# A graph-attention layer on one core: products and sums of a node group's end with one operand in PSUM

## The chip, the cores and the metric

The kernel runs on one core of one Trainium2 chip. The core has a matrix engine (TensorE, PE in the profile), a vector engine (VectorE, DVE), a scalar engine (ScalarE, ACT), a general engine (GpSimd, POOL) and a synchronisation engine (SyncE, SP) that issues most of the transfers. Each engine runs its own instructions in order; semaphores order the engines among themselves. SBUF is the working memory, PSUM the memory that TensorE writes its results to, in banks of 512 f32 columns on 128 partitions. GpSimd issues the indirect transfers, which fetch rows from main memory by a list of row numbers.

The metric is the device time of one execution in microseconds.

## The reference

12500 nodes with 128 features, 400000 edges sorted by destination, 8 heads of 16 channels. Cut to what matters:

```
h  = relu(layernorm(x))
xl, xr = ln(h) @ W_l, ln(h) @ W_r
m  = leaky_relu(xl[src] + xr[dst] + edge_attr @ W_e, 0.2)     # edges and one self loop for each node
alpha = sum(m * att, over the channels of a head)
a  = softmax of alpha over the edges of one destination and head
h  = h + sum(a * xl[src], over those edges) + bias
ff = gelu(ln(h) @ W1 + b1) @ W2 + b2
out = x + h + ff
```

The self loop uses the mean of edge_attr over all edges in place of an edge's own.

## The kernel before, in words

A first stage (lines 334 to 376) goes over 14 groups of seven node tiles, writes xl and xr to main memory and keeps h in SBUF (`h_sb`), with the bias added.

The second stage (`window_edges`) goes over the edges. A unit is 256 edges, a pair two units, 512 edges; there are 782 pairs. The work is software-pipelined by hand: one pass of the loop at line 931 is a round, and in round r each stage function handles the pair r minus its offset (table at line 868). For one pair:

- `gather` (line 517): four indirect transfers on GpSimd's queue fetch 128 rows of xl each into `xs`, one of 12 row buffers. There are 3125 of them in all.
- `combine` (559 to 563): TensorE transposes the rows into `z` and adds the destinations' part and the edges' part.
- `slope`, `bend` (569, 574): the leaky ReLU, ScalarE and VectorE, result `m` in SBUF.
- `score` (580, 581): the negated scores into `ab`, with large values where an edge doesn't belong to a node.
- `lowest`, `weigh` (588, 599): the minimum on VectorE, then exponentials on ScalarE into `p`.
- `turn`, `keep_turned` (607, 612): p transposed by TensorE, copied by ScalarE.
- `collect` (621): weighted sums of rows into a PSUM tile `acc`.
- `own_heads` (630, 636) and `put` (643): each head's own columns, written as a record to the `state` arrays in main memory.

PSUM has eight banks, and the pool `ps2` uses them all: two each for z, ab, pt_ps and acc. A tile of a name takes the two banks of that name in turn. A stage that asks for a bank waits until the last reader of its previous holder is done.

The third part is the node groups' end. The 98 node tiles are cut into 25 groups, one of two tiles and 24 of four, so an instruction over a group has 128 partitions x 512 columns. When all edges of a group are done, its steps (table at line 893) run one or two to a round beside the edge pairs' stages, at the end of the round. A group starts at the earliest 23 rounds after the one before it; the first starts in round 199, the last in round 790, after all edges. `bank_of` (line 676) gives a step a bank of the ring `acc`. The steps that the change touches, in order:

- `f_den` (740): weights of the two state records and of the self loop, divided by their sum, into `wt` (SBUF).
- `f_out` (750): products, two of the records' sums by their weights (line 755) and one of the self loop's rows by theirs (759).
- `f_add` (765): the three products are added up (767, 768).
- `f_h` (770): the sum is added to h (772), and the load of x is issued on SP's queue (773).
- `f_stats`, `f_root`, `f_scale`, `f_turn`, `f_turned` (775 to 818): layer norm of h, transposed; at its end x gets b2 added (818).
- `f_up`, `f_gelu` (820 to 842): the first layer of the feed forward, in two halves.
- `f_x` (844): x gets h added (846).
- `f_down`, `f_store` (848 to 866): the second layer, x plus its result (863), and the store.

The order of the round at line 931: `early`, the pair stages in the order of their table, the loads of the edge mean, the group's steps, then loads and record writes. Each engine's queue has that order.

Of the kernel before, what the change touches and what calls it, by code (L numbers as in the profile page):

```python
# [13 lines left out]
F32 = mybir.dt.float32  # L14
# [7 lines left out]
P = 128  # L22
H = 8
C = P // H
# [21 lines left out]
GN = 4  # L46
# [47 lines left out]
def node_groups(nt):  # L94

    first = nt % GN
    return ([(0, first)] if first else []) + [(t, GN) for t in range(first, nt, GN)]
# [19 lines left out]
def tile_gnn(  # L117
# [261 lines left out]
    with tc.If(fast == 1) as cmp:  # L379
        window_edges(  # L380
            tc, n_edges, ea_t, NT, NE, NUE, ident, wer, we_z, negrep, diag, nid, farw, b2_r, w1_sb, w2_sb, cols,
            xl_dram, xl_t, xr_t, xs_dram, dc_dram, du_dram, state, x_t, out_t, h_sb, src_sb, first_sb,
        )
# [67 lines left out]
def window_edges(  # L451
# [9 lines left out]
    nc = tc.nc  # L461
    SP = mybir.EngineType.SP
    KP = UP * KU
    EPR = UP * U
    AHEAD = 4
# [17 lines left out]
    with ExitStack() as es:  # L483
# [4 lines left out]
        ps2 = es.enter_context(tc.tile_pool(name="e_ps2", bufs=2, space=PSUM))  # L488

        fin = es.enter_context(tc.tile_pool(name="e_fin", bufs=1))  # L490
# [155 lines left out]
        sums = [None] * NL  # L646
# [23 lines left out]
        groups = [{"t0": t, "n": n, "ts": slice(t, t + n)} for t, n in node_groups(NT)]  # L670

        def tiles(name, d, tag=None, bufs=1):
            d[name] = fin.tile([P, GN, P], F32, name=f"f_{name}", tag=tag or f"f_{name}", bufs=bufs)
            return d[name][:, 0 : d["n"]]

        def bank_of(d, name):
            d[name] = ps2.tile([P, EPR], F32, name="acc")
            return d[name]

        def f_load(d):  # L680
# [16 lines left out]
        def f_z(d):  # L697

            n, z = d["n"], bank_of(d, "z")
            for i in range(n):  # L700
                nc.tensor.matmul(
                    z[:, i * P : (i + 1) * P], d["xl"][:, i, 0:P], ident, start=(i == 0), stop=False, is_transpose=True
                )
            for i in range(n):
                nc.tensor.matmul(z[:, i * P : (i + 1) * P], d["xr"][:, i, :], ident, start=False, stop=(i == n - 1))
# [9 lines left out]
        def f_score(d):  # L715

            n, sc = d["n"], bank_of(d, "sc")
            for i in range(n):
                nc.tensor.matmul(
                    sc[:, i * H : (i + 1) * H], d["m"][:, i, :], negrep[:, 0, :], start=(i == 0), stop=(i == n - 1)  # L720
                )
# [18 lines left out]
        def f_den(d):  # L740
            n, wt = d["n"], d["wt"]
            ws = fin.tile([P, 2, GN * H], F32, name="f_ws")[:, :, 0 : n * H]
            nc.vector.tensor_mul(ws, wt[:, 0:2], d["sums"][:, :, :, C])
            den = fin.tile([P, GN * H], F32, name="f_den")[:, 0 : n * H]
            nc.vector.tensor_add(den, ws[:, 0], ws[:, 1])
            nc.vector.scalar_tensor_tensor(den, den, 1e-16, wt[:, 2], op0=OP.add, op1=OP.add)
            nc.vector.reciprocal(den, den)
            nc.vector.tensor_mul(wt, wt, den[:, None].to_broadcast([P, 3, n * H]))

        def f_out(d):  # L750
            n, wt = d["n"], d["wt"]
            o = fin.tile([P, 2, GN * H, C], F32, name="f_o", tag="big", bufs=3)
            d["o"] = o.rearrange("p s (t h) c -> p s t (h c)", h=H)[:, :, 0:n]
            for i in range(2):
                nc.vector.tensor_mul(
                    o[:, i, 0 : n * H], d["sums"][:, i, :, 0:C], wt[:, i, :, None].to_broadcast([P, n * H, C])
                )
            o2 = tiles("o2", d, "f_a")
            nc.vector.tensor_mul(
                o2.rearrange("p t (h c) -> p (t h) c", c=C),  # L760
                d["xo"][:, 0:n].rearrange("p t (h c) -> p (t h) c", c=C),
                wt[:, 2, :, None].to_broadcast([P, n * H, C]),
            )

        def f_add(d):
            o = d["o"]
            nc.vector.tensor_add(o[:, 0], o[:, 0], o[:, 1])
            nc.vector.tensor_add(o[:, 0], o[:, 0], d["o2"][:, 0 : d["n"]])

        def f_h(d):  # L770
            hb = h_sb[:, d["ts"], :]
            nc.vector.tensor_add(hb, hb, d["o"][:, 0])
            nc.sync.dma_start(tiles("x", d), x_t[:, d["ts"], :])

        def f_stats(d):
# [27 lines left out]
        def f_turn(d):  # L803
            tp = bank_of(d, "tp")
            for i in range(d["n"]):
                nc.tensor.transpose(tp[:, i * P : (i + 1) * P], d["hn"][:, i, :], ident)

        def f_turned(d):
            n = d["n"]
            nc.scalar.activation(  # L810
                tiles("hT", d, "f_d").rearrange("p t f -> p (t f)"),
                d["tp"][:, 0 : n * P],
                AF.Identity,
                bias=cols[:, 3:4],
                scale=cols[:, 2:3],
            )
            x = d["x"][:, 0:n]
            nc.vector.tensor_add(x, x, b2_r[:, None, :].to_broadcast([P, n, P]))

        def f_up(k):  # L820
            def up(d):
                n, u = d["n"], bank_of(d, f"u{k}")
                nc.tensor.matmul(  # L823
                    u[:, 0 : n * P],
                    w1_sb[:, k * P : (k + 1) * P],
                    d["hT"][:, 0:n].rearrange("p t f -> p (t f)"),
                    start=True,
                    stop=True,
                )

            return up

        def f_gelu(k):
            def gelu(d):
                n = d["n"]
                if k == 0:
                    d["gel"] = fin.tile([P, 2, GN * P], F32, name="gel", tag="big", bufs=3)
                nc.scalar.activation(
                    d["gel"][:, k, 0 : n * P], d[f"u{k}"][:, 0 : n * P], AF.Gelu, bias=cols[:, 5 + k : 6 + k]
                )  # L840

            return gelu

        def f_x(d):
            x = d["x"][:, 0 : d["n"]]
            nc.vector.tensor_add(x, x, h_sb[:, d["ts"], :])

        def f_down(d):
            y = bank_of(d, "y")
            for i in range(d["n"]):  # L850
                for k in range(2):
                    nc.tensor.matmul(  # L852
                        y[:, i * P : (i + 1) * P],
                        d["gel"][:, k, i * P : (i + 1) * P],
                        w2_sb[:, k, :],
                        start=(k == 0),
                        stop=(k == 1),
                    )

        def f_store(d):  # L860
            n = d["n"]
            y = tiles("yo", d, "f_b")
            nc.vector.tensor_add(
                y, d["x"][:, 0:n], d["y"][:, 0 : n * P].rearrange("p (t f) -> p t f", f=P)
            )
            nc.sync.dma_start(out_t[:, d["ts"], :], y)

        stages = (
# [20 lines left out]
            (3, mean),  # L889
        )  # L890
        SUM_STEP = 2
        early = ((18, f_gelu(1)),)
        steps = (
            (0, f_load),
            (1, f_order),
# [3 lines left out]
            (5, f_low),  # L899
            (6, f_exp),  # L900
            (7, f_den),
            (8, f_out),
            (9, f_add),
            (10, f_h),
            (11, f_stats),
            (12, f_root),
            (13, f_scale),
            (14, f_turn),
            (15, f_turned),
            (16, f_up(0)),  # L910
            (17, f_up(1)),
            (17, f_gelu(0)),
            (18, f_x),
            (19, f_down),
            (20, f_store),
        )
        GAP = 23
        last_round = n_pr + LATE + 2
# [5 lines left out]
        def in_round(r, table):  # L924
            for k, f in table:
                for d in groups:
                    if d["round"] + k == r:
                        f(d)

        with tc.manual_schedule():  # L930
            for r in range(-AHEAD, max(last_round, groups[-1]["round"] + 21)):
                in_round(r, early)
                for late, f in stages:
                    c = r - late
                    if 0 <= c < n_pr:
                        f(c)
                for late, f in sum_stages:
                    i, off = divmod(r - late, SUM_STEP)
                    if off == 0 and 0 <= i < NL:
                        f(i)  # L940
                in_round(r, steps)
                for late, f in late_stages:
                    c = r - late
                    if 0 <= c < n_pr:
                        f(c)
# [335 lines left out]
```

## Time and profile before

| | us |
|---|---|
| median of 3 runs | 4345.91 |
| lowest, highest | 4344.86, 4346.41 |
| the profiled execution's own time | 4342.05 |
| its span, first to last instruction | 4340.7 |

Mean granted TensorE clock in the span: 0.940.

What the engines are busy with in the stretch in which node groups and edge pairs run side by side (columns: stretch in us, its length, then busy us and count of PE, PE's weight loads, VectorE, ScalarE and GpSimd, the clock, the share of the transfer engines, GB/s):

```profile
1310.00:4282.00 2972.00, 2632.88 (x13704) 1831.05 (x13821) 1660.21 (x3624) 1328.46 (x2683) 2257.84 (x2324) 0.96 0.57 112
```

The vector instructions of the group's end, by line (count of full groups, busy us, mean ns of one, idle time before them):

```profile
L755 DVE TENSOR_TENSOR f_o<-st,f_wt 128x512 f32<-128x512 f32 x48 | 30.8, 682 | 0.0
...
L768 DVE TENSOR_TENSOR f_o<-f_o,f_o 128x512 f32<-128x512 f32 x24 | 16.6, 692 | 0.8
...
L818 DVE TENSOR_TENSOR f_x<-f_x,b_r 128x512 f32<-128x512 f32 x24 | 16.4, 684 | 0.0
L846 DVE TENSOR_TENSOR f_x<-f_x,h_sb 128x512 f32<-128x512 f32 x24 | 16.4, 683 | 0.0
L759 DVE TENSOR_TENSOR f_o<-f_xo,f_wt 128x512 f32<-128x512 f32 x24 | 16.4, 682 | 0.0
L772 DVE TENSOR_TENSOR h_sb<-h_sb,f_o 128x512 f32<-128x512 f32 x24 | 16.4, 681 | 0.0
```

Such a row reads: the source line, the engine, the operation, the tile written and the tiles read, their shape, the count; then the sum of durations, the mean of one, and how long the engine had been idle just before such instructions, with what ended that. Seven lines (one of them with two instructions a group) of some 0.68 us each make about 131 us of VectorE's 2453.7.

### The profile page before, as it was taken

What the parts mean: (1) busy time and instruction counts of PE and PEld (TensorE: products, weight loads), DVE (VectorE), ACT (ScalarE), POOL (GpSimd) and SP (SyncE); (2) the same over time, 40 slices, a digit from 0 to 9 for tenths busy, and PEclk for the clock granted to TensorE, in tenths of its full rate; (3) what the DMA queues carried; (4) which work ended last, traced back from release to release, by engine and by line L of the source; (5) the groups of instructions that cost most, each with busy time, mean ns of one, the idle gap of its engine ahead of it and who ended that gap; (6) DMA issues with size and microseconds to landing.
All of it is one profiled execution on the core that took longest, in us unless ns stands there. A gap on an engine that the chain in (4) does not pass through costs nothing.

```text
span 4340.7 us, 65036 instructions
## 1 busy us (share of the span) xinstructions
PE 3622.3 (83%) x18449; PEld 2499.6 (58%) x18571; DVE 2453.7 (57%) x5415; ACT 1837.8 (42%) x3826; POOL 3140.2 (72%) x3244
## 2 busy tenths in 40 slices
PE   0558888888888888889888889888888888888996
PEld 0335565556556556666666566566666665665664
DVE  4755665656665555555555555555555555555554
ACT  0643333333334444444444444444444444444443
POOL 0567777777777777777777777777777777777773
PEclk9768999999999999999999999999999999999998
DMA  7456766766665555565555555555555555555552
GB/s 193 142 158 143 161 150 156 152 153 157 150 151 104 118 112 112 112 119 111 113 111 115 115 102 113 117 112 119 113 113 119 110 112 110 110 112 108 110 114 60
DMA packets 644020, 538.41 MB, mean 124 GB/s; under 512 B 381797, under 2 KB 533605, under 8 KB 643413
## 3 DMA queue, kind: packets, MB, share of 16 engines
q1 hardware_dynamic: 512212, 299.56, 28.6%
q0 software_dynamic: 100000, 217.80, 28.6%
q10 hardware_dynamic: 31440, 16.80, 1.6%
q8 instruction: 152, 2.49, 0.2%
q14 instruction: 216, 1.76, 0.2%
HBM read 473.99 MB, written 59.76 MB: 123 GB/s over the span
## 4 chain that ended last, share of the span: by engine, by line
PE 40%; DMA 23%; POOL 20%; issue 12%; ACT 2%; ACTq 2%; DVE 2%; SPq 0%; POOLq 0%; DVEq 0%
DMA xs<-xl_dram,src_sb 22%; POOL xs L517 20%; PE z L563 9%; PE acc L621 8%; PE ab L581 6%; PE z L559 4%; PE pt_ps L607 4%; PE z L562 2%; PE lr L363 2%; ACTq L334 1%; PE ab L580 1%; PE acc L852 1%; PE acc L823 1%; ACT h_sb L348 0%; ACT xlr L364 0%
## 5 line engine op out<-in xcount | busy, mean ns | idle before, releaser
L517 POOL DMA_INDIRECT xs<-xl_dram,src_sb x3125 | 3015.1, 965 | 952.4 <-issue 800.9
L599 ACT ACTIVATE p<-ab,rec 128x256 f32<-128x256 f32 x1563 | 656.5, 471 | 1665.6 <-DVE rec L588 1650.2
L630 DVE TENSOR_TENSOR own<-acc,diag 128x272 f32<-128x272 f32 x782 | 344.9, 441 | 1451.9 <-PE acc L621 1437.9
L559 PE MATMUL z<-ident,xs 128*128 128x128 f32 x3125 | 595.5, 286 | 493.6 <-DMA xs<-xl_dram,src_sb 470.1
L559 PEld LDWEIGHTS z<-ident,xs 128*128 128x128 f32 x3125 | 406.9, 142 | 974.3 <-DMA xs<-xl_dram,src_sb 606.9
L621 PE MATMUL acc<-xs,pt 128*128 128x136 f32 x6250 | 891.1, 287 | 0.0
L563 PE MATMUL z<-ea,we_z 128*128 128x512 f32 x1564 | 865.4, 637 | 0.1
L621 PEld LDWEIGHTS acc<-xs,pt 128*128 128x128 f32 x6250 | 820.2, 199 | 0.0
L581 PE MATMUL ab<-m,negrep 128*128 128x512 f32 x1564 | 800.4, 593 | 6.3
L569 ACT ACTIVATE zs<-z 128x512 f32<-128x512 f32 x782 | 474.7, 607 | 519.8 <-PE z L563 517.0
L607 PEld LDWEIGHTS pt_ps<-ident,p 128*128 128x128 f32 x3125 | 421.5, 150 | 458.3 <-issue 426.2
L588 DVE TENSOR_REDUCE rec<-ab 128x2 f32<-128x512 f32 x781 | 540.9, 693 | 137.1 <-PE ab L581 130.0
L574 DVE TENSOR_TENSOR m<-z,zs 128x512 f32<-128x512 f32 x782 | 532.1, 680 | 58.3 <-ACT zs L569 58.1
L607 PE MATMUL pt_ps<-ident,p 128*128 128x128 f32 x3125 | 502.9, 287 | 1.5 <-ACT pt L612 1.5
L612 ACT COPY pt<-pt_ps 128x512 f32<-128x512 f32 x782 | 458.4, 586 | 0.0
L636 DVE TENSOR_REDUCE rec<-own 128x34 f32<-128x272 f32 x782 | 340.9, 436 | 26.6
L563 PEld LDWEIGHTS z<-ea,we_z 128*128 128x128 f32 x1564 | 314.8, 201 | 35.5
L581 PEld LDWEIGHTS ab<-m,negrep 128*128 128x128 f32 x1564 | 301.6, 193 | 37.4 <-issue 0.7
L562 PE MATMUL z<-ne,xrw 128*128 128x512 bf16 (+1 forms) x781 | 310.5, 398 | 0.0
L545 DVE TENSOR_SCALAR ne<-dlw,nid 112x512 bf16<-112x512 bf16 x782 | 288.2, 369 | 2.1 <-DMA dlw<-du_dram 2.1
L580 PE MATMUL ab<-ne,farw 128*128 128x512 bf16 x662 | 255.2, 385 | 0.0
L656 DVE TENSOR_REDUCE part<-ea_s 128x1 f32<-128x1024 f32 x98 | 118.4, 1208 | 0.0
(147 smaller groups left out, 1712.6 us busy)
## 6 DMA issues: line engine op xcount, KB each, us to landing
dlw<-dc_dram SPq DMA_DIRECT2D x196, 384.0 KB
ea<-in_ea_t SPq DMA_DIRECT2D x196, 256.0 KB
ea_s<-in_ea_t SPq DMA_DIRECT2D x98, 512.0 KB
xs<-xl_dram,src_sb POOLq DMA_INDIRECT x3125
state<-rec SPq DMA_DIRECT2D x1563, 9.0 KB
xrw<-xs_dram SPq DMA_DIRECT2D x782, 24.0 KB
state<-empty ACTq DMA_DIRECT2D x28, 504.0 KB
st<-state SPq DMA_DIRECT2D x48, 288.0 KB
```

Source lines behind the costliest of these rows:

```text
L517: nc.gpsimd.indirect_dma_start(out=xs[:, j, :], out_offset=None, in_=xl_dram, in_offset=bass.IndirectOffsetOnAxis(ap=src_sb[:, c * KP + j ...
L559: nc.tensor.matmul(z[:, j * P : (j + 1) * P], d["xs"][:, j, 0:P], ident, start=(j == 0), stop=False, is_transpose=True)
L562: nc.tensor.matmul(z[:, :e], xrw[c % NV], d["ne"][:, :e], start=False, stop=False)
L563: nc.tensor.matmul(z[:, :e], we_z[:, c % QP, :], d["ea"][:, :e], start=False, stop=True)
L569: nc.scalar.activation(d["zs"][:, :e], d["z"][:, :e], AF.Copy, scale=SLOPE)
L574: nc.vector.tensor_tensor(d["m"][:, :e], d["z"][:, :e], d["zs"][:, :e], op=OP.max)
L581: nc.tensor.matmul(ab[:, :e], negrep.rearrange("p n h -> p (n h)"), d["m"][:, :e], start=False, stop=True)
L588: nc.vector.tensor_reduce(d["rec"][:, :, CX], d["ab"].rearrange("p (u e) -> p u e", e=U), AX.X, OP.min)
L599: nc.scalar.activation(d["p"][:, us], d["ab"][:, us], AF.Exp, bias=d["rec"][:, i, CX:SH], scale=-1.0)
L607: nc.tensor.transpose(d["pt_ps"][:, js], d["p"][:, js], ident)
L612: nc.scalar.copy(d["pt"][:, :e], d["pt_ps"][:, :e])
L621: nc.tensor.matmul(d["acc"][:, i, :], d["pt"][:, j * P : (j + 1) * P], d["xs"][:, j, :], start=(j == js[0]), stop=(j == js[-1]),)
```

## The change

- The weights, divided by their sum, go to a tile `wp` in a bank of the ring acc and no longer back to `wt` in SBUF.
- The products are made by `part_out`, which reads the weights from `wp`. The first product goes into a tile `sum` in a bank of the ring ab, the second to SBUF, and is added to `sum`; the third goes to SBUF. The step `f_add` is gone: in `f_h` the third product is added to `sum`, and then `sum` to h.
- The adds of b2 and of h to x are gone from `f_turned` and from `f_x` (which is gone as well); in `f_store` the result of the second layer gets x added in its PSUM bank, then h in the same bank, and b2 on the way to the tile that is stored.
- All steps from `f_h` on, `f_down` and `f_store` among them, come one round earlier.
- The second product's SBUF tile `f_e` is new; the tile `f_o`, a third user of the three buffers "big", is gone.

```diff
-        def bank_of(d, name):
-            d[name] = ps2.tile([P, EPR], F32, name="acc")
+        def bank_of(d, name, ring="acc"):
+            d[name] = ps2.tile([P, EPR], F32, name=ring)
             return d[name]
...
-            nc.vector.tensor_mul(wt, wt, den[:, None].to_broadcast([P, 3, n * H]))
+            wp = bank_of(d, "wp")[:, 0 : 3 * GN * H].rearrange("p (s t) -> p s t", s=3)[:, :, 0 : n * H]
+            nc.vector.tensor_mul(wp, wt, den[:, None].to_broadcast([P, 3, n * H]))
+            d["wp"] = wp
+
+        def part_out(d, i, out):
+            n = d["n"]
+            a = d["xo"][:, 0:n].rearrange("p t (h c) -> p (t h) c", c=C) if i == 2 else d["sums"][:, i, :, 0:C]
+            nc.vector.tensor_mul(
+                out.rearrange("p (t c) -> p t c", c=C), a, d["wp"][:, i, :, None].to_broadcast([P, n * H, C])
+            )
 
         def f_out(d):
-            n, wt = d["n"], d["wt"]
-            o = fin.tile([P, 2, GN * H, C], F32, name="f_o", tag="big", bufs=3)
...
-        def f_add(d):
-            o = d["o"]
-            nc.vector.tensor_add(o[:, 0], o[:, 0], o[:, 1])
-            nc.vector.tensor_add(o[:, 0], o[:, 0], d["o2"][:, 0 : d["n"]])
+            n = d["n"]
+            d["sum"] = bank_of(d, "sum", "ab")[:, 0 : n * P]
+            part_out(d, 0, d["sum"])
+            o = tiles("o", d, "f_e").rearrange("p t f -> p (t f)")
+            part_out(d, 1, o)
+            nc.vector.tensor_add(d["sum"], d["sum"], o)
+            d["o2"] = tiles("o2", d, "f_a").rearrange("p t f -> p (t f)")
+            part_out(d, 2, d["o2"])
 
         def f_h(d):
-            hb = h_sb[:, d["ts"], :]
-            nc.vector.tensor_add(hb, hb, d["o"][:, 0])
+            hb = h_sb[:, d["ts"], :].rearrange("p t f -> p (t f)")
+            nc.vector.tensor_add(d["sum"], d["sum"], d["o2"])
+            nc.vector.tensor_add(hb, hb, d["sum"])
             nc.sync.dma_start(tiles("x", d), x_t[:, d["ts"], :])
...
-            x = d["x"][:, 0:n]
-            nc.vector.tensor_add(x, x, b2_r[:, None, :].to_broadcast([P, n, P]))
...
-        def f_x(d):
-            x = d["x"][:, 0 : d["n"]]
-            nc.vector.tensor_add(x, x, h_sb[:, d["ts"], :])
...
-            nc.vector.tensor_add(
-                y, d["x"][:, 0:n], d["y"][:, 0 : n * P].rearrange("p (t f) -> p t f", f=P)
-            )
+            up = d["y"][:, 0 : n * P].rearrange("p (t f) -> p t f", f=P)
+            nc.vector.tensor_add(up, up, d["x"][:, 0:n])
+            nc.vector.tensor_add(up, up, h_sb[:, d["ts"], :])
+            nc.vector.tensor_add(y, up, b2_r[:, None, :].to_broadcast([P, n, P]))
             nc.sync.dma_start(out_t[:, d["ts"], :], y)
...
-        early = ((18, f_gelu(1)),)
+        early = ((17, f_gelu(1)),)
...
-            (9, f_add),
-            (10, f_h),
-            (11, f_stats),
-            (12, f_root),
-            (13, f_scale),
-            (14, f_turn),
-            (15, f_turned),
-            (16, f_up(0)),
-            (17, f_up(1)),
-            (17, f_gelu(0)),
-            (18, f_x),
-            (19, f_down),
-            (20, f_store),
+            (9, f_h),
+            (10, f_stats),
+            (11, f_root),
+            (12, f_scale),
+            (13, f_turn),
+            (14, f_turned),
+            (15, f_up(0)),
+            (16, f_up(1)),
+            (16, f_gelu(0)),
+            (18, f_down),
+            (19, f_store),
```

More of the change, by code (lines that the diff above doesn't have):

```diff
@@ L747, in f_den @@
             nc.vector.reciprocal(den, den)
-            nc.vector.tensor_mul(wt, wt, den[:, None].to_broadcast([P, 3, n * H]))
-        def f_out(d):
-            n, wt = d["n"], d["wt"]
-            o = fin.tile([P, 2, GN * H, C], F32, name="f_o", tag="big", bufs=3)
[L753 to L756, printed above, removed]
-                )
[L758 to L763, printed above, removed]
-        def f_add(d):
-            o = d["o"]
-            nc.vector.tensor_add(o[:, 0], o[:, 0], o[:, 1])
-            nc.vector.tensor_add(o[:, 0], o[:, 0], d["o2"][:, 0 : d["n"]])
+            wp = bank_of(d, "wp")[:, 0 : 3 * GN * H].rearrange("p (s t) -> p s t", s=3)[:, :, 0 : n * H]
[7 more added lines that the diff above has]
+            )
+        def f_out(d):
+            n = d["n"]
[6 more added lines that the diff above has]
+            part_out(d, 2, d["o2"])
         def f_h(d):
-            hb = h_sb[:, d["ts"], :]
-            nc.vector.tensor_add(hb, hb, d["o"][:, 0])
+            hb = h_sb[:, d["ts"], :].rearrange("p t f -> p (t f)")
+            nc.vector.tensor_add(d["sum"], d["sum"], d["o2"])
+            nc.vector.tensor_add(hb, hb, d["sum"])
             nc.sync.dma_start(tiles("x", d), x_t[:, d["ts"], :])
@@ L862, in f_store @@
             y = tiles("yo", d, "f_b")
-            nc.vector.tensor_add(
-                y, d["x"][:, 0:n], d["y"][:, 0 : n * P].rearrange("p (t f) -> p t f", f=P)
-            )
+            up = d["y"][:, 0 : n * P].rearrange("p (t f) -> p t f", f=P)
+            nc.vector.tensor_add(up, up, d["x"][:, 0:n])
+            nc.vector.tensor_add(up, up, h_sb[:, d["ts"], :])
+            nc.vector.tensor_add(y, up, b2_r[:, None, :].to_broadcast([P, n, P]))
             nc.sync.dma_start(out_t[:, d["ts"], :], y)
@@ L930, in window_edges @@
         with tc.manual_schedule():
-            for r in range(-AHEAD, max(last_round, groups[-1]["round"] + 21)):
+            for r in range(-AHEAD, max(last_round, groups[-1]["round"] + 20)):
                 in_round(r, early)
```

## The prediction

> **What bounds the kernel now.** I read the page's busy shares first. TensorE is the busiest engine, and a reader might stop there:
>
> ```profile
> PE 3622.3 (83%) x18449; PEld 2499.6 (58%) x18571; DVE 2453.7 (57%) x5415; ACT 1837.8 (42%) x3826; POOL 3140.2 (72%) x3244
> ...
> L517 POOL DMA_INDIRECT xs<-xl_dram,src_sb x3125 | 3015.1, 965 | 952.4 <-issue 800.9
> ```
>
> But look at the gathers' row (busy, mean ns, idle before): 3125 gathers have 952.4 us of idle time before them, 0.305 us each, and the view of that one line says what this idle time is:
>
> ```profile
> L517 POOL DMA_INDIRECT xs<-xl_dram,src_sb x3125: 940/944/2885, 308.7 to 4275.0; - x196
> ...
>   issue: 800.9, 2628
> ```
>
> The shortest and the median gather are alike (940 and 944 ns) and one took 2885. In the timeline every gap between two gathers lies between 0.303 and 0.317 us, so POOL never waits for anybody: it issues from 308.7 us to the end of the last gather, 4276.0, without a pause. That stretch is 3967.3 us = 3015.1 + 952.2. **POOL's chain of gathers sets the time**, with 308.7 us ahead of it and 4340.7 - 4276.0 = 64.7 us behind. TensorE follows: it waits for gathered rows in the waits view (470.1 and 606.9 us before line 559), and in the timeline's last stretch, where rows are there already, a round takes it 3.95 us (line 580 at 4242.97, 4246.92, 4250.87, 4254.82) where POOL needs 4 x 1.249 = 5.00.
>
> Now the 944 against the mean of 965: 3015.1 - 3125 x 0.944 = 65.1 us of gathers that took longer than they need. Where? By stretch (time, POOL's busy us and count, clock, DMA share, GB/s), before the first node group's end and after it:
>
> ```profile
> 320.00:1310.00 990.00, 748.55 (x792) 0.95 0.68 153
> 1310.00:4282.00 2972.00, 2257.84 (x2324) 0.96 0.57 112
> ```
>
> 0.945 us each while DMA moves 153 GB/s, 0.972 each later at 112 GB/s: it isn't the memory traffic, it comes with the groups. The timeline of one group (start, duration, engine, line, instruction) shows the partner:
>
> ```profile
> 2174.54 0.94 POOL L517 DMA_INDIRECT xs<-xl_dram,src_sb  x1 [0.30 <-issue]
> ...
> 2174.99 0.68 DVE L574 TENSOR_TENSOR m<-z,zs 128x512 f32<-128x512 f32 x1
> ...
> 2175.80 2.77 POOL L517 DMA_INDIRECT xs<-xl_dram,src_sb  x1 [0.31 <-issue]
> 2175.85 1.28 DVE L755 TENSOR_TENSOR f_o<-st,f_wt 128x512 f32<-128x512 f32 x2
> ...
> 2177.05 0.68 DVE L759 TENSOR_TENSOR f_o<-f_xo,f_wt 128x512 f32<-128x512 f32 x1
> ...
> 2179.96 0.69 DVE L767 TENSOR_TENSOR f_o<-f_o 128x512 f32<-128x512 f32 x1
> ...
> 2180.12 1.35 POOL L517 DMA_INDIRECT xs<-xl_dram,src_sb  x1 [0.30 <-issue]
> ```
>
> A gather beside line 574, which has one operand in PSUM, takes 0.94. Beside lines 755 and 759, both operands in SBUF, it takes 2.77 and ends about where they end. Laying every gather over every VectorE instruction in the trace: the 144 gathers that overlap lines 755, 759, 767, 768, 772, 818 or 846 hold **60.2 us** of the excess (35.0 of it beside the products 755 and 759, 25.2 beside the sums); the other 2981 hold 4.8. The 1175 gathers that overlap only lines 574, 588, 630 and 636 (one PSUM operand, or a reduction) have a mean of 0.944, though nearly all of these 781 rounds overlap one.
>
> **The change, part by part.**
>
> *Removed: VectorE instructions with two large SBUF operands.* All seven lines get one operand in PSUM: the products read the weights from there, the sums run in a PSUM tile, and the two adds on x move to the store, with the product of the second layer as PSUM operand. No 128x512 instruction with two SBUF inputs is left in a group's end. If one PSUM operand does for them what it does for lines 574 and 630, the 60.2 us go. The short ones that stay (lines 732, 743, and line 748's successor, 96 columns) carry about 1 us, line 545 alone beside a gather 3.0 (52 gathers); they are in the 4.8.
>
> [...] The trace has 60.2, and I take it: these are indirect gathers, and the row that matters is their own.
>
> *Cost of a PSUM operand.* [...]
>
> ```profile
> L863 DVE TENSOR_TENSOR f_yo<-f_x,acc 128x512 f32<-128x512 f32 x24 | 16.5, 688 | 14.2 <-PE acc L852 14.2
> L767 DVE TENSOR_TENSOR f_o<-f_o 128x512 f32<-128x512 f32 x24 | 16.4, 684 | 0.0
> ```
>
> 688 against 684: 4 ns, 1 us in all by the row. [...] I take 0. The count of instructions in a group doesn't change: 10 before, 10 after.
>
> *Added waits.* The sum takes a buffer of the ring of two that line 581's result (ab) uses, so in the round of the products VectorE's first product waits for ScalarE's exponentials (line 599) of that round. In the trace line 755 starts 0.16 us before those end: about 0.2 us, with the rest of VectorE's queue behind it. One round later TensorE's score (line 580) must wait for line 599 of its own round, which waits for line 588, queued behind the products on VectorE; behind score stand the next round's transposes. In all 24 groups of the trace that run beside gathers line 599 ended 1.1 to 8.9 us before the score of that round began, so I take no wait. Likewise collect (line 621) now waits for the last product, which ended at least 2.3 us ahead of it. The store's two further adds end 1.37 us later, and collect of the next round, which needs that buffer, began 1.06 us after the one add: 0.3 us of TensorE per group. All this is covered: TensorE has 5.00 - 3.95 = 1.05 us in each of 23 rounds, 24 us per group, less about 9 for the group's own matmuls: 15 us. If that cover goes, each us counts. POOL itself is held only when row buffers run out: 12 of them, of which six rounds plus the gather lead are in use; the constant gaps show it never came near.
>
> *Moved.* From the weights on, steps come a round earlier, so the x load on SP's queue goes a round or so earlier between state writes, and the whole stands one round shorter. While gathers run this is beside POOL's chain. Nothing is issued more or less.
>
> *The tail.* After the last gather the last group runs alone, in sequence. Products and sums are six instructions before and after. But lines 818 and 846 ran beside TensorE and ScalarE there, and now two adds stand between the last matmul and the store: 2 x 0.70 = **+1.4 us**. How far TensorE lags at the last gather varies by about 3 us either way (its round began 1.2 to 6.8 us after the gather in the last eight pairs).
>
> **Sum.** 308.7 + (3967.3 - 60.2) + 64.7 + 1.4 = 4281.9 of span, 1.35 outside it: 4283.2 against the profiled 4342.05, so -58.8. The runs' median, 4345.91, stands 3.9 above the profiled execution; the same difference puts the forecast at **4287**.
>
> **Rivals.**
>
> 1. [...] The products read the sums with a stride of 18 from SBUF, and nothing in the trace pairs that with PSUM. If they still block, only the 25.2 us go: 4345.9 - 25.2 + 1.4 = 4322. If only the products are cured, 35.0: 4312. Against it: lines 630 and 574 are clean with PSUM on one side. 8 in 100.
>
> 2. [...] 4 in 100.
>
> 3. *Slower: the ring of two ab buffers.* Score waits for exponentials that wait for VectorE that waited for the previous exponentials: a loop around three engines. It decides once it costs TensorE more than its 15 us per group, and makes the kernel slower than before from 15 + 2.5 = 17.5 us, 4.4 TensorE rounds, per group. At 20 us per group: (20 - 17.5) x 24 = 60 us, 4406. Against it: the margins above, 1.1 us at worst. 4 in 100.
>
> The forecast has the remaining 84.
>
> **Range.** For the likeliest case: new forms or other phases may keep 10 us of contention, or all 65.1 go; 3 us for the tail: 4277 to 4300. Up to 4312 it holds half of rival 1. So 4276 to 4312. Within 0.2% means within 8.7 us, about what a measurement of this kernel can tell from none: faster 0.92 (forecast and rival 1), same 0.04, slower 0.04.
>
> **What would show it.** The L517 row: about 2955 us, mean 946, its maximum far below 2.8 us, gaps still 0.305, and the last gather starting near 4215. VectorE's busy time within 10 us of 2453.7. TensorE's waits for rows smaller or equal, no large new wait of line 580 on line 599. It is wrong if long gathers remain beside the new products, if POOL's gaps grow (buffers run out, so TensorE became the bound), or if the stretch after the last gather grows by more than some 5 us.

## The result, and the profile after

| | before | after |
|---|---|---|
| median of the runs, us | 4345.39 (4342.7 to 4346.41, 4 runs) | 4286.18 (4285.17 to 4288.52, 4 runs) |
| the profiled execution's own time | 4342.05 | 4285.49 |
| its span | 4340.7 | 4283.3 |

The ratio of after to before is 0.9865 (95% interval 0.985 to 0.9879): 59 us less.

The page of the changed kernel, its busy shares and the gathers' row (count, busy us, mean ns, idle before), and below them that line's own view (shortest, median and longest gather in ns, first and last start):

```profile
PE 3613.1 (84%) x18425; PEld 2501.6 (58%) x18571; DVE 2462.2 (57%) x5415; ACT 1831.4 (43%) x3826; POOL 3081.4 (72%) x3244
...
L517 POOL DMA_INDIRECT xs<-xl_dram,src_sb x3125 | 2956.2, 946 | 952.4 <-issue 803.4
```

```profile
L517 POOL DMA_INDIRECT xs<-xl_dram,src_sb x3125: 940/944/1210, 309.4 to 4217.0; - x196
```

The gathers' busy time fell from 3015.1 to 2956.2, by 58.9 us; the idle time between them is 952.4 as before, so POOL still runs without a pause; the longest gather is 1210 ns, where it was 2885. The last one starts 58.0 us earlier. By stretch, first without and then with node groups beside the gathers:

```profile
320.00:1310.00 990.00, 748.72 (x792) 0.95 0.68 153
1310.00:4222.00 2912.00, 2199.37 (x2325) 0.95 0.59 114
```

0.945 and 0.946 us a gather: the second stretch had 0.972. And one group's products and their neighbours in the timeline:

```profile
2157.09 0.95 POOL L517 DMA_INDIRECT xs<-xl_dram,src_sb  x1 [0.30 <-issue]
2157.78 0.70 DVE L756 TENSOR_TENSOR ab<-st,acc 128x512 f32<-128x512 f32 x1
2158.34 0.94 POOL L517 DMA_INDIRECT xs<-xl_dram,src_sb  x1 [0.30 <-issue]
2158.39 0.68 DVE L756 TENSOR_TENSOR f_o<-st,acc 128x512 f32<-128x512 f32 x1
2159.11 0.70 DVE L766 TENSOR_TENSOR ab<-ab,f_o 128x512 f32<-128x512 f32 x1
2159.59 0.95 POOL L517 DMA_INDIRECT xs<-xl_dram,src_sb  x1 [0.30 <-issue]
2159.71 0.68 DVE L756 TENSOR_TENSOR f_o<-f_xo,acc 128x512 f32<-128x512 f32 x1
```

Three gathers begin before and beside the products, and none is longer than 0.95 us.

### The profile page after: what moved, and what is told of

The parts are those of the page before. It is cut to its first block, busy times and chain, and to the rows that moved or that the text cites. A ratio compares the mean times of both kernels' runs of the same rounds, so it can differ in the third digit from the quotient of the medians.

```text
span 4283.3 us, 65055 instructions
## 1 busy us (share of the span) xinstructions
PE 3613.1 (84%) x18425; PEld 2501.6 (58%) x18571; DVE 2462.2 (57%) x5415; ACT 1831.4 (43%) x3826; POOL 3081.4 (72%) x3244
## 4 chain that ended last, share of the span: by engine, by line
PE 40%; DMA 24%; POOL 20%; issue 11%; ACT 2%; DVE 2%; ACTq 1%; POOLq 0%; SPq 0%; DVEq 0%
DMA xs<-xl_dram,src_sb 23%; POOL xs L517 20%; PE z L563 9%; PE acc L621 8%; PE ab L581 6%; PE z L559 4%; PE pt_ps L607 4%; PE z L562 2%; PE lr L363 2%; ACTq L334 1%; PE ab L580 1%; PE acc L847 1%; PE acc L822 1%; ACT h_sb L348 1%; ACT xlr L364 0%
## 5 line engine op out<-in xcount | busy, mean ns | idle before, releaser
L517 POOL DMA_INDIRECT xs<-xl_dram,src_sb x3125 | 2956.2, 946 | 952.4 <-issue 803.4
L559 PE MATMUL z<-ident,xs 128*128 128x128 f32 x3125 | 587.7, 286 | 440.2 <-DMA xs<-xl_dram,src_sb 412.8
L559 PEld LDWEIGHTS z<-ident,xs 128*128 128x128 f32 x3125 | 406.9, 142 | 912.6 <-DMA xs<-xl_dram,src_sb 536.8
L563 PEld LDWEIGHTS z<-ea,we_z 128*128 128x128 f32 x1564 | 315.5, 202 | 35.8
L580 PE MATMUL ab<-ne,farw 128*128 128x512 bf16 x638 | 246.6, 387 | 0.0
```

The source lines that it names most:

```text
L517: nc.gpsimd.indirect_dma_start(out=xs[:, j, :], out_offset=None, in_=xl_dram, in_offset=bass.IndirectOffsetOnAxis(ap=src_sb[:, c * KP + j ...
L559: nc.tensor.matmul(z[:, j * P : (j + 1) * P], d["xs"][:, j, 0:P], ident, start=(j == 0), stop=False, is_transpose=True)
L563: nc.tensor.matmul(z[:, :e], we_z[:, c % QP, :], d["ea"][:, :e], start=False, stop=True)
```

## The experiments

Nine kernels, twelve runs. The "excess" of a run is the busy time of its L517 row less 3125 x 0.944 us: 65.1 before, 6.2 after. A gather is called held by a VectorE instruction that makes it longer. All are edits of the changed kernel; its median, 4286.18, is what they stand against, and each ratio is against runs of the kernel before on the same chip.

### All operands back in SBUF, the earlier steps kept

```diff
-            wp = bank_of(d, "wp")[:, 0 : 3 * GN * H].rearrange("p (s t) -> p s t", s=3)[:, :, 0 : n * H]
-            nc.vector.tensor_mul(wp, wt, den[:, None].to_broadcast([P, 3, n * H]))
-            d["wp"] = wp
+            nc.vector.tensor_mul(wt, wt, den[:, None].to_broadcast([P, 3, n * H]))
+            d["wp"] = wt
...
-            d["sum"] = bank_of(d, "sum", "ab")[:, 0 : n * P]
+            d["sum"] = tiles("sum", d, "f_sum").rearrange("p t f -> p (t f)")
...
-            nc.vector.tensor_add(up, up, d["x"][:, 0:n])
-            nc.vector.tensor_add(up, up, h_sb[:, d["ts"], :])
-            nc.vector.tensor_add(y, up, b2_r[:, None, :].to_broadcast([P, n, P]))
+            x = d["x"][:, 0:n]
+            nc.vector.tensor_add(x, x, b2_r[:, None, :].to_broadcast([P, n, P]))
+            nc.vector.tensor_add(x, x, h_sb[:, d["ts"], :])
+            nc.vector.tensor_add(y, x, up)
```

> The changed kernel's steps, one round earlier, but every product and sum with both operands in SBUF again (weights and sum in SBUF tiles; at the store x gets b2 and h, then the layer's product). If the gathers are held by VectorE instructions with two SBUF inputs, the whole stall is back: 60 us of long gathers, mean of the L517 row 964 to 966, time 4340 to 4350. If the earlier steps or the step that is gone brought the gain, the time stays near 4286 and the row near 946.

### Products alone, sums alone

The second kernel has the second and third of these edits only (weights in PSUM, sums in SBUF); the third has the first only (weights in SBUF, sums in PSUM).

> Only the three products read their weights from PSUM; all sums have two SBUF operands. By the account of the trace before (35.0 us of long gathers beside the products, 25.2 beside the sums) the gathers keep 25 us of the stall: L517 mean 953 to 955, time about 4312, between 4304 and 4320. If only PSUM results or the sums matter: 4340 or more.

> Only the sums and the adds at the store have a PSUM operand; the products read both operands from SBUF, the first of them writing to PSUM. If two SBUF inputs hold the gathers, wherever the result goes, 35 us of the stall stay: time about 4321, 4314 to 4330, and gathers of more than 2 us remain beside the products. If a result in PSUM frees an instruction as well, a third of the products' part goes: about 4309. If sums don't matter: 4340 or more.

These three ran on a chip on which the kernel before took 5055.21 us, and gave 5039.08, 5040.71 and 5042.66 (0.9969, 0.9968 and 0.9971, with intervals no wider than 0.9955 to 0.9983). As times they tell nothing of the theories: their gathers were busy 2999.4, 2977.6 and 2957.8 us, which is 42 us of difference, and the times don't follow. Their chain of waits shows why; this is the first one's:

```profile
PE 71%; issue 14%; another core or an unknown queue 5%; DVE 4%; ACT 2%; ACTq 1%; DMA 1%; POOL 1%; SPq 0%; POOLq 0%; DVEq 0%
...
L517 POOL DMA_INDIRECT xs<-xl_dram,src_sb x3125 | 2999.4, 960 | 1649.6 <-issue 826.4
```

POOL is 1% of the chain there, where it was 20% before, and its idle time is 1649.6 us and not 952.4: in part (268.1 us) it waits until line 621 is done with a row buffer, in part (328.1) for something that the trace doesn't name. TensorE sets the time on that chip, with waits inside its own queue; why is open. The clock granted there was 0.907, against 0.945 in the same kernel's run further down: 4% less, where the time is 17% longer. So the same kernels ran again elsewhere, where the kernel before took 4342.53 us:

> The kernel of e1_sbuf, to be had on a chip on which POOL's gathers set the time (the run before was on one where the kernel before took 5055 us and TensorE was late). Its own trace there held 49 us of long gathers in place of 6. Two SBUF inputs hold the gathers: 4325 to 4350. The earlier steps brought the gain: near 4286.

> The kernel of e2_products, products with PSUM weights, sums with two SBUF operands. From its trace on the slow chip, 27.6 us of long gathers, 21 more than in the changed kernel: 4307, between 4300 and 4316. From the trace before, 25.2: 4311.

> The kernel of e3_sums, sums with PSUM, products with two SBUF operands. The forecast on record from the trace before was 4321 (35 us stay). From its trace on the slow chip, only 7.8 us of long gathers: a gather was held only until the end of the first product, not of the second, and the third stood alone at a place where no gather began. If that holds here: 4285 to 4294.

| kernel | median, us | ratio (95% interval) | excess, us |
|---|---|---|---|
| all in SBUF | 4321.93 | 0.9953 (0.9936 to 0.9969) | 44.3 |
| products alone with PSUM | 4300.15 | 0.9907 (0.9891 to 0.9924) | 23.1 |
| sums alone with PSUM | 4291.84 | 0.9883 (0.9866 to 0.9899) | 8.8 |

The operands count and not the earlier steps: with the steps alone the kernel is 35.8 us slower than the changed one, and the excess accounts for it (44.3 - 6.2 = 38.1). But the sizes missed. All in SBUF, 44.3 us of the 65.1 came back and not all, a little below the 4325 to 4350 expected. With two SBUF operands in the products alone (the table's third row), 2.6 us more than in the changed kernel are left of the 35.0 that stood beside them in the kernel before: the first forecast, 4321, was 29 us too high, and only the second, made from its own trace on the other chip, held. With two SBUF operands in the sums alone (the second row): 4300.15, at the edge of 4300 to 4316, below the first forecast of 4312. The two parts don't add up, 16.9 + 2.6 us against 38.1. The timelines show what decides. This is the kernel with everything in SBUF:

```profile
2517.87 0.34 DVE L545 TENSOR_SCALAR ne<-dlw,nid 112x512 bf16<-112x512 bf16 x1
2517.98 2.25 POOL L517 DMA_INDIRECT xs<-xl_dram,src_sb  x1 [0.30 <-issue]
2518.12 0.69 DVE L755 TENSOR_TENSOR f_sum<-st,f_wt 128x512 f32<-128x512 f32 x1
2518.73 0.68 DVE L755 TENSOR_TENSOR f_o<-st,f_wt 128x512 f32<-128x512 f32 x1
2519.45 0.69 DVE L765 TENSOR_TENSOR f_sum<-f_sum,f_o 128x512 f32<-128x512 f32 x1
```

The gather ends at 2520.23, 0.82 us after the end of the second product (2519.41), though a third instruction with two SBUF inputs, the sum, runs by then: the sum waited for the product, and the gather got in. In the kernel before, the three products stood in a row without a wait, and the gather shown in the prediction ended 0.83 us after the third. In both, the instruction that was running as the gather began was not a product but line 545, a VectorE instruction of every edge round with one tensor input; here is the line for the kernel before:

```profile
2175.59 0.34 DVE L545 TENSOR_SCALAR ne<-dlw,nid 112x512 bf16<-112x512 bf16 x1
```

The first product began 0.14 and 0.05 us into the gather, before line 545 was over, and took the hold on. Sorted by what was running as they began, 20 of the held gathers of the kernel before, with 21.4 of the 60.2 us, were held by line 545 first and then by the product, sum or add that followed it without a pause, the seven longest among them. The change leaves line 545 as it is. In the changed kernel 78 gathers are still held by it to its own end, for 5.7 us in all, and four to the end of the short line 743 behind it, for 0.9. No 128x512 instruction takes its hold on there: each has an operand in PSUM.

And with sums in PSUM and products in SBUF:

```profile
2163.78 0.96 POOL L517 DMA_INDIRECT xs<-xl_dram,src_sb  x1 [0.30 <-issue]
2164.03 0.70 DVE L755 TENSOR_TENSOR ab<-st,f_wt 128x512 f32<-128x512 f32 x1
2164.64 0.68 DVE L755 TENSOR_TENSOR f_o<-st,f_wt 128x512 f32<-128x512 f32 x1
2165.05 1.09 POOL L517 DMA_INDIRECT xs<-xl_dram,src_sb  x1 [0.31 <-issue]
```

Here the first product, whose result goes to PSUM, began 0.25 us into a gather and cost it 0.02; the second gather began in the second product's course and ended, again, 0.82 us after it. So in these traces a gather is longer when such an instruction is running as it begins, here by 0.15 us: it ends 0.82 us after the end of that instruction, and in some rows of instructions after that of a later one.

### The cost by itself

One or two instructions more in each of the 782 rounds, behind line 574; their results are not used.

```diff
             nc.vector.tensor_tensor(d["m"][:, :e], d["z"][:, :e], d["zs"][:, :e], op=OP.max)
+            junk = work.tile([P, EPR], F32, name="junk", bufs=2)
+            nc.vector.tensor_tensor(junk[:, :e], d["m"][:, :e], d["zs"][:, :e], op=OP.max)
```

> The changed kernel with one more VectorE maximum of 128x512 in each of the 782 rounds, both inputs in SBUF, its result not used. If such an instruction holds a gather that meets it, at 0.15 to 0.33 us each as the lone sums did in the kernel before, 120 to 260 us more: 4400 to 4545, L517 mean up by 38 to 83 ns. If VectorE's time in the round is what counts, the same as with one operand in PSUM (its sibling run).

The sibling reads `d["z"]`, which is in PSUM, in place of `d["m"]`:

> The same extra maximum, its first input z in PSUM and the second in SBUF. VectorE does 0.68 us more in each round, 530 us in all, but no gather is held: 4280 to 4295, L517 mean 945 to 947. If VectorE's time or its queue is what counted, or TensorE's slack is smaller than worked out, slower than 4300.

A third has `nc.vector.tensor_copy(junk[:, :e], d["zs"][:, :e])` there:

> The same place, an f32 copy of 128x512 from SBUF to SBUF: one input only. If a second tensor input is what holds the gathers, nothing: near 4286, L517 mean 946. [...]

And a fourth has the first one's maximum twice, into the same tile:

> Two of the extra maxima with two SBUF inputs, one right after the other, in each round. [...] If each costs its own share alone, twice the extra of its sibling run with one.

| extra in each round | median, us | ratio (95% interval) | excess, us |
|---|---|---|---|
| maximum, two SBUF inputs | 4377.66 | 1.0082 (1.0064 to 1.01) | 91.2 |
| maximum, one input in PSUM | 4286.45 | 0.9871 (0.9854 to 0.9887) | 5.0 |
| copy, SBUF to SBUF | 4331.05 | 0.9967 (0.9954 to 0.9979) | 52.7 |
| two maxima, two SBUF inputs | 4409.66 | 1.0148 (1.0131 to 1.0165) | 137.9 |

The edits of the first two differ in the memory of one operand alone. Their rows, first with two SBUF inputs and then with one in PSUM:

```profile
L576 DVE TENSOR_TENSOR junk<-m,zs 128x512 f32<-128x512 f32 x781 | 542.7, 695 | 27.0
```

```profile
L576 DVE TENSOR_TENSOR junk<-z,zs 128x512 f32<-128x512 f32 x781 | 531.8, 681 | 0.0
```

and their gathers, in the same order:

```profile
L517 POOL DMA_INDIRECT xs<-xl_dram,src_sb x3125 | 3041.2, 973 | 952.5 <-issue 802.5
```

```profile
L517 POOL DMA_INDIRECT xs<-xl_dram,src_sb x3125 | 2955.0, 946 | 952.3 <-issue 801.8
```

With an input in PSUM, 532 us more of VectorE cost nothing: 4286.45 against 4286.18. With both in SBUF they cost 91 us, though VectorE's own time is nearly the same. The first also waits for line 574's result (27.0 us of idle time) and the second doesn't, but that isn't it: of the second's gathers, 300 began 0.08 to 0.56 us after its maximum, and they were longer by 0.000 us in the mean; all 323 that began so in the first were longer. This settles that it is the memory of one input that counts, and that VectorE's time had cover. The 91 are less than the 120 to 260 expected, and two maxima cost 1.4 times one (123.5 against 91.5) where twice was expected if each costs its own share. The main cause of both misses is the same, and the trace of the first shows it when every gather is sorted by where the maximum started, relative to the gather's own start (means over the gathers of each bin):

| maximum starts, us after the gather | gathers | longer by, us | gather ends after the maximum, us |
|---|---|---|---|
| -0.64 to -0.56 | 53 | 0.000 | 0.86 |
| -0.48 to -0.40 | 50 | 0.123 | 0.82 |
| -0.32 to -0.24 | 40 | 0.294 | 0.82 |
| -0.16 to -0.08 | 37 | 0.452 | 0.82 |
| 0.00 to 0.08 | 48 | 0.000 | 0.20 |
| 0.16 to 0.24 | 57 | -0.001 | 0.05 |

By this table one point of the gather counts, by estimate 0.944 - 0.82 = 0.12 us after its start. A maximum that began 0.08 us or more before the gather and still ran at that point delayed the rest of it, by 0.123 to 0.452 us in three of the rows; one that ended earlier, or began later, delayed nothing (0.000, 0.000 and -0.001 us in the other three). By what means, no trace shows. And a held gather waited for one maximum only, not for the two of the fourth kernel: the longest gather is 1462 ns in both. Two such places in the timeline of the first kernel, the first gather held for 0.44 us and the second not at all:

```profile
2461.29 0.69 DVE L576 TENSOR_TENSOR junk<-m,zs 128x512 f32<-128x512 f32 x1
2461.42 1.38 POOL L517 DMA_INDIRECT xs<-xl_dram,src_sb  x1 [0.30 <-issue]
...
2500.76 0.94 POOL L517 DMA_INDIRECT xs<-xl_dram,src_sb  x1 [0.30 <-issue]
2500.84 0.69 DVE L576 TENSOR_TENSOR junk<-m,zs 128x512 f32<-128x512 f32 x1
```

The longest delay is thus 1.462 - 0.944 = 0.52 us, and a gather begins every 1.25 us. At random phases a maximum of 0.69 us then costs, by estimate, 0.5 x 0.52 x 0.52 / 1.25 = 0.11 us; measured (91.2 - 6.2) / 782 = 0.109. The phases are not always even: where a round has two maxima one after the other, the first held 313 gathers for 82.3 us in all and the second 253 for 55.8.

The copy, with one input, costs 45 us as well: a single SBUF source doesn't make an instruction harmless. In its trace 33.0 us of the excess end 0.82 us after a copy; 14.8 stand beside line 545 alone, which met more gathers than in the changed kernel (5.7). The copy of 512 columns takes 0.44 us, well below line 574's 0.68.

### Two in a row without a wait

Two maxima into two tiles, so that the second doesn't wait for the first; then two products in the form of the kernel's own.

```diff
+            for i in range(2):
+                junk = work.tile([P, EPR], F32, name=f"junk{i}", bufs=1)
+                nc.vector.tensor_tensor(junk[:, :e], d["m"][:, :e], d["zs"][:, :e], op=OP.max)
```

> The changed kernel with two extra maxima with two SBUF inputs per round, as in d4_twice, but into two tiles, so that the second doesn't wait for the first. In d1 a gather was held only if the maximum ran when it began, and ended 0.82 us after the maximum's end. If two without a wait between hold the gather as one of 1.3 us: 0.5 x 1.13 x 1.13 / 1.25 = 0.51 us per round, 400 us more than the changed kernel, 4600 to 4780. If the gather gets in between them as in d4_twice: 4400 to 4460.

```diff
...
+                nc.vector.tensor_mul(
+                    junk[:, :e].rearrange("p (t c) -> p t c", c=C), d["m"][:, :e].rearrange("p (t c) -> p t c", c=C),
+                    d["zs"][:, 0 : e // C, None].to_broadcast([P, e // C, C]),
+                )
```

> As f1_in_a_row, two extra instructions with two SBUF inputs in each round and no wait between them, but products whose second input is one column spread over 16, the form that the kernel's own products have. In f1 a gather was let in after the first; in the kernel before it was held to the end of the third product. If the spread second input is what lets the hold pass from one instruction to the next: about 0.51 us per round, 400 us more than the changed kernel, 4600 to 4780, with gathers up to 2 us. If not, as f1: 4450 to 4490, no gather over 1.5 us.

4471.09 us (1.0293, 1.0276 to 1.031) and 4464.25 (1.029, 1.0272 to 1.0308), excess 194.3 and 180.0: 2.2 and 2.0 times what a single one added. The first is above the 4400 to 4460 expected for a gather that gets in, and far below the 4600 of the other case; the second is in the range of that case. From the timeline of the first:

```profile
2152.38 1.29 DVE L577 TENSOR_TENSOR junk<-m,zs 128x512 f32<-128x512 f32 x2
2152.49 1.40 POOL L517 DMA_INDIRECT xs<-xl_dram,src_sb  x1 [0.31 <-issue]
```

The pair runs until 2153.67, the gather ends at 2153.89: 0.82 after the end of the first maximum (about 2153.07), not of the pair; of some 330 gathers held by the first maximum, none was held on by the second. So a missing wait between the two isn't enough to pass the hold on, and the spread second input isn't either. Why the three products of the kernel before held the gather to the end of the third (every one that met the first or second), and the pair in the all-SBUF kernel to the end of the second, **stays open**. A difference not tried: there no instruction of the row waited, while here the first of the two waited for line 574's result. It is unlikely to be the whole answer. The second maximum, which didn't wait, passed nothing on to line 545 behind it (some 310 gathers). And in the kernel with only the sums in PSUM, four of the first products followed line 545 without a pause, and the gathers that they held got in at their end; but their result goes to PSUM, which may matter.

## Why the prediction was right, by its steps

**What bounds the kernel.** Right. With the same gaps and shorter gathers the time fell by what the gathers lost: the span by 57.4 us, of 58.9 less 0.7 more ahead of the first gather and 0.7 more behind the last. And 532 us more of VectorE changed nothing. It holds where the kernel before takes some 4345 us: on the chip where TensorE was late, 42 us of gathers bought nothing.

**60.2 us of the excess go.** 58.9 went. In the changed kernel no gather that meets the new products or sums is longer by more than 0.12 us, and what is left, 6.2 us, stands beside line 545 and the small instructions, forecast at 4.8. The lines that the prediction named were not the only holders: it read the gather of 2.77 us as one held by the products that ends about where they end; it was held by line 545 first, and it ends 0.83 us after them. The 60.2 came out all the same, because every 128x512 instruction that took a hold on from line 545 was on one of the seven lines that were changed. Taking the trace's own row for these gathers was right: two SBUF inputs cost them 91 us in the experiment, and an input in PSUM nothing (4286.45 against 4286.18). But two SBUF inputs are not the only condition: line 545 and the copy, with one tensor input each, held gathers too, for 5.7 us in the changed kernel and 33.0 in the copy's. Nor did the experiment's maximum cost its whole length: of its 0.69 us a round the gathers lost 0.109.

**The split into products and sums**, on which rival 1 was built, was wrong. 35.0 and 25.2 us described where the gathers were long in that one arrangement. The products alone cost 2.6 us over the changed kernel's excess and the sums alone 16.9, because it matters what stands behind what and where it meets a gather. The step that failed took overlap in a trace for the price of an instruction; no run has the kernel before with only its products cured, so the 4312 of that rival wasn't tried as such.

**Cost of a PSUM operand.** The rows after: products with weights in PSUM 680 and 677 ns into SBUF and 696 into PSUM, sums 687 to 700, where all took 681 to 692. Summed over all groups, the durations of the lines in question rose by 1.8 us, near the row's 1. The prediction took 0 of it for the kernel's time, and 532 us more of VectorE cost nothing in the experiment. VectorE's busy time rose by 8.5 us, inside the 10 forecast, and mostly for another reason: some 5 us of it are instructions that no longer overlap the one before.

```profile
L859 DVE TENSOR_TENSOR acc<-acc,f_x 128x512 f32<-128x512 f32 x24 | 16.8, 700 | 14.6 <-PE acc L847 13.7 <-issue 0.7
...
L756 DVE TENSOR_TENSOR ab<-st,acc 128x512 f32<-128x512 f32 x24 | 16.7, 696 | 2.0
...
L756 DVE TENSOR_TENSOR f_o<-f_xo,acc 128x512 f32<-128x512 f32 x24 | 16.2, 677 | 0.0
```

A result of 512 columns in PSUM, which no VectorE row of the trace before has, cost the first product 16 to 19 ns against the other two.

**Added waits.** None shows. In the waits view TensorE's waits around the score come to this, of 4283 us:

```profile
PEld z L559 <- PE ab L581: 7.6, 7, 1.6
...
PEld z L559 <- DVE ab L772: 1.2, 5, 0.2
```

There is no entry of lines 580 and 581 waiting for line 599. TensorE's waits for rows fell from 470.1 and 606.9 to 412.8 and 536.8: it follows the gathers, with less room. That 15 us per group is the point from which a wait costs was not tried.

**The tail.** 66.1 us forecast after the last gather, 65.4 measured; the three adds at its end are in the timeline as worked out, 0.70, 0.70 and 0.69 us. The forecast of 4287 was 0.8 us off, and that is luck: for the profiled execution the same sum gave 4283.2, and 4285.49 was measured.

## What to carry to other kernels

Where indirect gathers issued by GpSimd set the pace, compare their longest and mean duration with their median, and look in the timeline for the VectorE instruction that was running when a long one began. Look also at what ran just before it: the holder can be an instruction that hands its hold on, as line 545 did here in 21.4 of the 60.2 us. Moving one operand to PSUM made VectorE's instructions 1.8 us longer here, all groups together, and the gathers 58.9 us shorter. It pays only where GpSimd's queue is the bound: first see that its gaps are constant (0.303 to 0.317 us here), for on the chip where TensorE was late 42 us of gathers bought nothing. Don't price a part of such a contention by its overlap: it depends on phases, and the parts didn't add up (16.9 + 2.6 us against 38.1).

## What the runs showed that was not expected

- A gather was sensitive at one point only, by estimate 0.12 us after its start. A maximum with two SBUF inputs that started in its course cost it 0.000 us, and so did one that had ended by that point; a product or sum that started in its course and took on the hold of line 545 made it up to 2885 ns long. The end of a held gather was 0.81 to 0.83 us after the end of what held it last, in the kernel before, in the changed one and in the experiments' timelines above alike.
- A row of such instructions held a gather as one (line 545 and three products, to the end of the third: up to 2885 ns), or let it in after the first (two maxima: the longest gather took 1472 ns); what decides between the two wasn't found.
- A plain f32 copy from SBUF to SBUF of 443 ns in each round made the kernel 45 us slower; 33.0 us of held gathers stand beside the copies themselves, 0.04 us each.
- The same program can have another bound on another chip: 5055 us before, with TensorE 71% of the chain in the kernel with all operands in SBUF. The three kernels that ran there gained 0.3% each, however long their gathers were; the changed kernel itself did not run there.
